# Mamba times mixture of experts: the second expert's rows are weighed and added by one VectorE operation

## The chip, the cores and the metric

The kernel runs on one core of a Trainium2 chip. The core has five engines with a queue each, which work in order and wait for one another by semaphores: PE (TensorE, matrix products), DVE (VectorE), ACT (ScalarE), POOL (GpSimd) and SP (SyncE, which here only issues DMAs). The metric is the device time in microseconds of one execution; less is better. Before the change it is 1489.96 us, the median of three runs from 1489.83 to 1492.37.

## The reference

For 4096 tokens (2 x 2048) of width 256 the reference computes, with everything in fp32:

```
xn = layernorm(x)
s  = xn + mamba(rmsnorm(xn));  s = s + silu(rmsnorm(s) @ w1.T) @ w2.T   # mamba scan, then an MLP
p  = softmax(xn @ gate_w + gate_b); the two best of 8 experts by token
e  = p[first] * expert_first(xn) + p[second] * expert_second(xn)        # relu MLPs, 256-1024-256
out = x + s * silu(e)
```

The Mamba part holds a recurrence over time, h = h * dA + (dt * u) * B, for 512 channels and 16 states, and sums h * C over the states. What matters here is the line with e: two rows of expert output by token, each times its probability, added, and silu of the sum as a gate.

## The kernel before, in words

The tokens are cut into 8 blocks (c) of 512. The Mamba part runs in 256 steps n: for each block 4 groups of 128 channels (d) and 8 pairs of states (g). A step has two half-steps, one state each. In a step VectorE makes b = du * B for both states (L1498) and runs one scan in each half-step (L1502, h); ScalarE makes da by exp for the step two further on (L1387); GpSimd multiplies h by C (L1430) and for most steps adds the two states (L1432); PE adds the result into y three steps later (L1400). At the start of a group VectorE makes du = dt * xc (L1495), with both inputs in SBUF and the output in PSUM.

Everything else is laid between these half-steps. PE's side work (the experts, then the MLP in pieces of 256 tokens) is drawn by an estimate of its time, a fixed amount for each half-step. The evacuations that follow are put off by a list called `later`: `later.put(work, after=k)` runs the work k half-steps on (one without k), and works of the same half-step run in the order in which they were put. So the order on each engine is settled when the program is written, and an engine that stands at a wait holds back all that is behind it.

The experts' outputs lie in DRAM as ys_d. For each of the 16 pieces of 256 tokens of the MLP, `gather` fetches the two rows of each token: four indirect DMAs on GpSimd's queue (L1185), j for the half of the tokens, k for first or second expert, into yk[0] and yk[1], both in SBUF. Five half-steps later `weigh` multiplies the four parts by their probabilities on ScalarE (L1199) and adds yk[1] to yk[0] on GpSimd (L1203). Seven half-steps after the gather `tanh` puts tanh of the half sum into yk[1] on ScalarE (L1207; `prob` already holds the factor one half). At the end of the piece `finish` adds the MLP's product po, in PSUM, to its input (L1218, L1220) and then, in `end`, forms (tanh + 1) * po * yk[0] + x in three VectorE operations (L1228, L1229, L1230; xom is the output piece), which also frees the PSUM bank "o" for PE's next product (pom of the next MLP piece, or po of the Mamba output, L821).

`act_table` (L183) loads ScalarE's table of functions when another than the present one is asked for. exp and tanh share one here; silu has its own. The MLP's silus are gathered (`silus`, L1144) so as to switch less. In the last block the own copy of `yk`, called ykm in the profile, serves the very last piece.

Of the kernel before, what the change touches and what calls it, by code (L numbers as in the profile page):

```python
# [10 lines left out]
AF = mybir.ActivationFunctionType  # L11
ALU = mybir.AluOpType
# [4 lines left out]
NE, FF, TOPK = 8, 1024, 2  # L17
# [11 lines left out]
JS = TS // P  # L29
# [23 lines left out]
def kernel(  # L53
# [18 lines left out]
    nc = tc.nc  # L72
# [107 lines left out]
    def act_table(name):  # L180

        if table[0] != name:
            nc.scalar.preload_act_table_set(name)  # L183
            table[0] = name
# [25 lines left out]
    prob = keep.tile([P, TOPK, NI], F32, tag="prob", name="prob")  # L210
# [145 lines left out]
    later = Later()  # L356
# [19 lines left out]
    def ring(tag, bufs):  # L376

        n = take(tag)
        later.free(tag, n - bufs)
        return tag, n  # L380
# [700 lines left out]
    class Mlp(Ffn):  # L1081
# [82 lines left out]
        def gather(self):  # L1164

            c, hf = self.c, self.hf
            i0 = c * J + hf * JS
            if self.own:
                yk_own = [
                    rows.tile([P, JS, DM], F32, tag="yk", name=f"yk{self.name}_{k}")  # L1170
                    for k in range(TOPK)
                ]
            else:
                yk_taken.append(self.name)
            if not yk_tiles:
                for k in range(TOPK):
                    yk_tiles.append(
                        wpool.tile([P, JS, DM], F32, tag=f"w{k + 1}", name=f"yk{k}", bufs=5)
                    )
            yk = self.yk = yk_own if self.own else yk_tiles  # L1180
            for no in expert_rows:
                later.free(*no)
            for j in range(JS):
                for k in range(TOPK):
                    nc.gpsimd.indirect_dma_start(  # L1185
                        out=yk[k][:, j, :], out_offset=None, in_=ys_d,
                        in_offset=bass.IndirectOffsetOnAxis(
                            ap=row_y[:, k, i0 + j : i0 + j + 1], axis=0
                        ),
                    )  # L1190
            self.nxo = ring("ys", 2)
            self.xo = rows.tile([P, JS, DM], F32, tag="ys", name=f"xo{self.name}")
            self.tok = slice(c * T + hf * TS, c * T + (hf + 1) * TS)
            nc.sync.dma_start(self.xo, x[self.tok, :].rearrange("(j p) d -> p j d", p=P))

            def weigh():
                for j in range(JS):
                    for k in range(TOPK):
                        nc.scalar.activation(  # L1199
                            yk[k][:, j, :], yk[k][:, j, :], AF.Copy,  # L1200
                            scale=prob[:, k, i0 + j : i0 + j + 1],
                        )
                nc.gpsimd.tensor_tensor(yk[0], yk[0], yk[1], ALU.add)  # L1203

            def tanh():
                act_table(WITH_TANH)
                nc.scalar.activation(yk[1], yk[0], AF.Tanh)  # L1207
                self.gated = True

            later.put(weigh, after=5)  # L1210
            later.put(tanh, after=7)

        def finish(self, po, n):
            x1, yk, xo = self.x1, self.yk, self.xo
# [371 lines left out]
```

## Time and profile before

| what | value |
|---|---|
| median of 3 runs | 1489.96 us |
| profiled execution | 1505.4 us, span of its instructions 1503.7 us |
| granted TensorE clock, mean | 0.944 |
| PE, DVE, ACT, POOL busy over the span | 90%, 81%, 65%, 79% |
| first gather of expert rows, last one | 1065.1 us, 1438.6 us |
| ACT table loads | 121 of 1.283 us |
| weighing on ACT (L1199) | 64 operations, 0.50 us each |
| adding on POOL (L1203) | 16 operations, 1.27 us each |
| tanh of the sum on ACT (L1207) | 16 operations, 0.63 us each |

An entry such as "POOL TENSOR_TENSOR h<-h,C 128x1024" names the engine, the operation, the tile written and the tiles read, and the shape as partitions by elements. In rows of groups the number after the bar is busy time in us, then the mean of one in ns, then the idle time of the engine before them and who ended it. In rows of waits the three numbers are us in total, times, and the longest. In rows of the timeline come start, duration, and in brackets the idle time before.

### The profile page before, as it was taken

To read this page: it belongs to the slowest core of one execution; us is meant where nothing else is said; L and a number is where in the kernel's file an instruction comes from. 1 tells how busy PE (TensorE), PEld (TensorE's weight loads), DVE (VectorE), ACT (ScalarE), POOL (GpSimd) and SP (SyncE) were. 2 spreads that over 40 slices of the span, in tenths; PEclk is the share of its full clock that TensorE was granted. 3 is DMA by queue.
4 is the path that set the end of the run, shared out by engine and by line. 5 is a ranking of instruction groups with operands and counts; after the bars stand their busy time and mean duration, and the time that the engine had idled before them with its cause. 6 is when DMAs were issued, how large, how long until landed. Compare 5 with 4: busy or idle time off the path is not lost.

```text
span 1503.7 us, 18025 instructions
## 1 busy us (share of the span) xinstructions
PE 1347.4 (90%) x5122; PEld 944.1 (63%) x5122; DVE 1217.2 (81%) x1351; ACT 978.5 (65%) x1765; POOL 1188.3 (79%) x964
## 2 busy tenths in 40 slices
PE   5744799999999999999999999979878998999958
PEld 4531467765776677766776677546655666667726
DVE  7448888889798998799888988999767967888853
ACT  4742777458655776568656865677648988778932
POOL 2665779987898799968997899889975888777860
PEclk9556899999999999999999999999999999999989
DMA  5568134962477345924492449445830116412110
GB/s 187 198 234 304 46 99 145 306 220 76 125 230 280 92 131 180 335 95 121 158 363 74 129 140 331 167 139 175 268 114 8 55 53 211 139 53 60 57 57 14
DMA packets 169317, 231.85 MB, mean 154 GB/s; under 512 B 19825, under 2 KB 139761, under 8 KB 169217
## 3 DMA queue, kind: packets, MB, share of 16 engines
q1 hardware_dynamic: 163072, 213.91, 42.9%
q0 software_dynamic: 6144, 16.79, 3.4%
q8 instruction: 41, 0.67, 0.2%
q14 instruction: 60, 0.48, 0.1%
HBM read 195.12 MB, written 35.52 MB: 153 GB/s over the span
## 4 chain that ended last, share of the span: by engine, by line
PE 44%; POOL 25%; DVE 10%; ACT 10%; issue 6%; DMA 4%; another core or an unknown queue 1%; POOLq 0%; DVEq 0%; SPq 0%; ACTq 0%
POOL h L1430 13%; PE phe L946 9%; PE y L1400 8%; PE poe L958 8%; POOL h L1432 6%; PE pom L958 4%; PE phm L946 4%; PE po L821 3%; ACT L183 2%; PE px L621 2%; DVE h L1502 2%; DMA B<-bcd 2%; ACT da L1387 2%; PE pz L772 2%; DMA C<-bcd 1%
## 5 line engine op out<-in xcount | busy, mean ns | idle before, releaser
L1430 POOL TENSOR_TENSOR h<-h,C 128x1024 f32<-128x1024 f32 x255 | 604.1, 2371 | 36.7 <-issue 11.5
L1502 DVE TENSOR_TENSOR_SCAN h<-da,hs,b 128x512 f32<-128x512 f32 x384 | 477.6, 1270 | 41.4 <-PE y L1400 10.8
L1387 ACT ACTIVATE da<-dt,a_neg 128x512 f32<-128x512 f32 x512 | 352.8, 717 | 93.3 <-DVE h L1502 87.2
L1400 PE MATMUL y<-h,ident 128*128 128x512 f32 x596 | 307.3, 617 | 34.6 <-POOL h L1432 17.5
L1498 DVE TENSOR_TENSOR b<-du,B 128x1024 f32<-128x1024 f32 x256 | 315.0, 1231 | 18.4 <-DMA B<-bcd 9.1
L1432 POOL TENSOR_TENSOR h<-h 128x512 f32<-128x512 f32 x214 | 275.4, 1287 | 16.8
L946 PE MATMUL phe<-xsTe,w_e 128*128 128x256 f32 (+1 forms) x1248 | 268.1, 366 | 9.4 <-ACT xsTe L937 7.6
L946 PEld LDWEIGHTS phe<-xsTe,w_e 128*128 128x128 f32 x1248 | 225.4, 194 | 72.7 <-issue 27.6
L958 PE MATMUL poe<-w_e,hide 128*128 128x256 f32 x1136 | 265.2, 380 | 2.5 <-ACT hide L1053 2.5
L958 PEld LDWEIGHTS poe<-w_e,hide 128*128 128x128 f32 x1136 | 213.8, 190 | 65.1 <-issue 33.5
L1053 ACT ACTIVATE hide<-phe,b 128x256 f32<-128x256 f32 (+1 forms) x312 | 123.6, 450 | 140.8 <-PE phe L946 140.4
L1400 PEld LDWEIGHTS y<-h,ident 128*128 128x128 f32 x596 | 112.2, 197 | 124.0 <-issue 60.5
L1502 DVE TENSOR_TENSOR_SCAN h<-da,b 128x512 f32<-128x512 f32 x128 | 151.3, 1210 | 12.7 <-PE y L1400 4.8
L183 ACT ACT_TABLE_LOAD x121 | 155.2, 1283 | 2.9 <-PEq L1573 0.8
L946 PE MATMUL phm<-xsTm,w_m 128*128 128x256 f32 x512 | 121.0, 387 | 2.7 <-ACT hidm L1144 2.0
L1424 POOL COPY hs<-h 128x2 f32<-128x2 f32 x192 | 42.0, 219 | 100.9 <-DVE h L1502 89.4
L958 PE MATMUL pom<-w_m,hidm 128*128 128x256 f32 x512 | 121.0, 386 | 0.0
L946 PEld LDWEIGHTS phm<-xsTm,w_m 128*128 128x128 f32 x512 | 99.1, 194 | 29.6 <-issue 10.8
L958 PEld LDWEIGHTS pom<-w_m,hidm 128*128 128x128 f32 x512 | 98.5, 194 | 25.2 <-issue 12.5
L462 POOL DMA_INDIRECT xs_d<-xt,slot x64 | 64.0, 1000 | 49.1 <-issue 21.4
L646 DVE SCALAR_TENSOR_TENSOR xc<-px,par_sb,xc 128x512 f32<-128x512 f32 x96 | 71.6, 748 | 30.4 <-ACT xc L638 25.6
L1185 POOL DMA_INDIRECT yk<-ys_d,row_y x60 | 58.3, 972 | 22.6 <-issue 14.2
(221 smaller groups left out, 1366.7 us busy)
## 6 DMA issues: line engine op xcount, KB each, us to landing
w_e<-in_w SPq DMA_DIRECT2D x312, 256.0 KB
B<-bcd SPq DMA_DIRECT2D x64, 512.0 KB
C<-bcd SPq DMA_DIRECT2D x64, 512.0 KB
xs<-xs_d SPq DMA_DIRECT2D x32, 256.0 KB
ys_d<-ys SPq DMA_DIRECT2D x32, 256.0 KB
b<-in_b SPq DMA_DIRECT2D x39, 128.0 KB
xnr<-xnd SPq DMA_DIRECT2D x16, 256.0 KB
xom<-in_x SPq DMA_DIRECT2D x16, 256.0 KB
```

Source lines behind the costliest of these rows:

```text
L183: nc.scalar.preload_act_table_set(name)
L462: r = nc.gpsimd.indirect_dma_start(out=xs_d, out_offset=bass.IndirectOffsetOnAxis(ap=slot[:, k, i : i + 1], axis=0), in_=x_of(i // J, i % ...
L646: nc.vector.scalar_tensor_tensor(v[:, s : s + T], px, conv_w[:, d, KC - 1 - s : KC - s], v[:, s : s + T], ALU.mult, ALU.add,)
L946: nc.tensor.matmul(ph[:, q, :], self.w1[c0 // 2][:, k, ts(q, P)], self.xT[:, k, :], start=(k == 0), stop=(k == KM - 1),)
L958: nc.tensor.matmul(po[:, j, :], self.hid[c // 2][:, c % 2, ts(j, P)], self.w2[c // 2][:, c % 2, :], start=(c == 0 and j == 0), stop=(c == ...
L1053: nc.scalar.activation(hc[:, q, :], ph[:, q, :], AF.Relu, bias=self.b1[:, c0 + q : c0 + q + 1])
L1387: nc.scalar.activation(das[n][:, q, :], dts[c, d], AF.Exp, scale=a_neg[:, d, 2 * g + q : 2 * g + q + 1])
L1400: nc.tensor.matmul(ys[c, d], ident, hts[n][:, q, :], start=False, stop=(g == DS // 2 - 1 and q == nq - 1),)
L1430: engine.tensor_tensor(hts[n], hts[n], bct[c, "C", g], ALU.mult)
L1432: nc.gpsimd.tensor_tensor(hts[n][:, 0, :], hts[n][:, 0, :], hts[n][:, 1, :], ALU.add)
L1498: nc.vector.tensor_tensor(inp, dus[c, d].unsqueeze(1).to_broadcast([P, 2, T]), bct[c, "B", g], ALU.mult,)
L1502: nc.vector.tensor_tensor_scan(hts[n][:, q, :], das[n][:, q, :], inp[:, q, :], 0.0 if c % CPB == 0 else hs[c - 1][:, d, 2 * g + q : 2 * g ...
```

## The change

`weigh` now multiplies only the first expert's rows on ScalarE. Half a step later a new work `join` multiplies the second expert's rows by their probability and adds them to the first's, in one VectorE operation for each half of the tokens; GpSimd's add is gone. `join` then puts `tanh`, which so runs in the half-step after it. By count that is the same half-step as before, but since it is put later it comes behind other works of that half-step.

```diff
             def weigh():
                 for j in range(JS):
-                    for k in range(TOPK):
-                        nc.scalar.activation(
-                            yk[k][:, j, :], yk[k][:, j, :], AF.Copy,
-                            scale=prob[:, k, i0 + j : i0 + j + 1],
-                        )
-                nc.gpsimd.tensor_tensor(yk[0], yk[0], yk[1], ALU.add)
+                    nc.scalar.activation(
+                        yk[0][:, j, :], yk[0][:, j, :], AF.Copy,
+                        scale=prob[:, 0, i0 + j : i0 + j + 1],
+                    )
+                later.put(join)
+
+            def join():
+                for j in range(JS):
+                    nc.vector.scalar_tensor_tensor(
+                        yk[0][:, j, :], yk[1][:, j, :], prob[:, 1, i0 + j : i0 + j + 1],
+                        yk[0][:, j, :], ALU.mult, ALU.add,
+                    )
+                later.put(tanh)
 
             def tanh():
                 act_table(WITH_TANH)
@@
             later.put(weigh, after=5)
-            later.put(tanh, after=7)
```

The sixteen gathers then carry 32 weighings on ScalarE, 32 operations on VectorE and none on GpSimd. In the built program the order on PE and on SP is unchanged; ScalarE's order differs, beside the 32 missing weighings, at two gathers (the 10th and the 15th), and has two table loads more.

## The prediction

> **What bounds the kernel now.** I read the engine shares and the chain that ended last first, then busy time by stretch, since shares over the whole span mix stages. Only the last third counts: the sixteen gathers of expert rows start at 1065 us.
>
> ```profile
> PE 1347.4 (90%) x5122; PEld 944.1 (63%) x5122; DVE 1217.2 (81%) x1351; ACT 978.5 (65%) x1765; POOL 1188.3 (79%) x964
> 1065.00:1440.00 375.00, 342.93 (x1278) 240.43 (x1276) 297.16 (x282) 295.63 (x454) 297.91 (x235) 0.97 0.30 98
> 1460.00:1503.70 43.70, 33.13 (x145) 27.69 (x144) 14.70 (x29) 11.45 (x27) 0.00 (x0) 0.95 0.04 12
> ```
>
> The numbers behind each stretch are PE, PE weight loads, DVE, ACT, POOL. From 1065 to 1440 PE is busy 91%, the other three 79% each: no engine rules the stretch, the chain changes hands. Only PE's 32 us of idle time, and the tail in which PE waits for POOL, can give anything back. The waits of that stretch say who holds whom:
>
> ```profile
> DVE pom L1218 <- PE pom L958: 24.6, 11, 6.4
> ACT yk L1207 <- POOL yk L1203: 21.7, 10, 6.2
> POOL yk L1203 <- ACT yk L1199: 13.1, 7, 5.9
> PE po L821 <- DVE xom L1230: 10.6, 3, 6.1
> ```
>
> One ring: ScalarE weighs (L1199), GpSimd adds (L1203), ScalarE takes tanh (L1207), VectorE multiplies (L1228), and PE's next product waits for the bank. VectorE itself waits 24.6 us for PE: this is its slack.
>
> **The change part by part.** The working groups of the rows, from the lists by tile and by line:
>
> ```profile
> L1199 ACT ACTIVATE yk<-yk,prob x60: 491/496/510, 1069.8 to 1442.6; 128x256 f32<-128x256 f32 x60
> L1203 POOL TENSOR_TENSOR yk<-yk,yk x15: 1262/1275/1282, 1077.8 to 1451.4; 128x512 f32<-128x512 f32 x15
> L1495 DVE TENSOR_TENSOR du<-dt,xc x32: 673/982/2885, 93.0 to 1407.4; 128x512 f32<-128x512 f32 x32
> L1066 DVE TENSOR_TENSOR ys<-poe,b 128x256 f32<-128x256 f32 x7 | 2.9, 411 | 0.6 <-PE poe L958 0.6
> L567 DVE SCALAR_TENSOR_TENSOR scratch<-scratch,ends x1: 2272/2272/2272, 136.9 to 136.9; 128x8 f32<-128x8 f32 x1
> ```
>
> Removed: 16 GpSimd adds of 1.275 us, 20.4 us of POOL; 32 of 64 ScalarE weighings, and since four overlap to 1.70 us and two to 0.90, 0.80 us a gather, 12.8 us of ACT. Added: 32 VectorE operations on 128x256. The built order of PE and of SP is the same line for line; the gathers keep their places on POOL's queue. So no transfer and no matmul moves by order.
>
> *Price of the VectorE operation.* By L1066 it is 0.41 us. But L1066 reads one operand from PSUM, and the new operation reads both from SBUF. The kernel's recurring VectorE work otherwise avoids that (b, the scan and pom have a PSUM operand); the exception is du, L1495, and its row spreads from 673 to 2885 ns. The longest one beside GpSimd:
>
> ```profile
> 413.85 2.88 DVE L1495 TENSOR_TENSOR du<-dt,xc 128x512 f32<-128x512 f32 x1
> ...
> 413.81 2.37 POOL L1430 TENSOR_TENSOR h<-h,C 128x1024 f32<-128x1024 f32 x1
> 416.26 1.60 POOL L1432 TENSOR_TENSOR h<-h 128x512 f32<-128x512 f32 x1
> ```
>
> du ends 0.55 us after the GpSimd operation that it met, and the next GpSimd operation takes 1.60 for its usual 1.27. L567, a scalar_tensor_tensor of 8 columns, took 2.27 us for the same reason. The Trainium skill (SBUF — State Buffer, "Who interferes with whom") says that a VectorE instruction with two SBUF inputs contends with a GpSimd instruction that reads SBUF and that one fully blocks. That speaks against this change. By the bare row (0.41) the 32 operations cost 13 us of VectorE; by the rule at its worst, each behind a whole 2.37 us operation, 32 x 2.8 = 90 us. The row decides between: du's mean over 32 is 1129 (36.1/32), 0.46 above its undisturbed 0.67. I take 0.41 + 0.46 = 0.87 each, 1.74 a gather, 28 us of VectorE in all. What no row shows is the second of a pair directly after the first: it may pass at once (0.41) or wait for the GpSimd operation queued meanwhile (up to 2.4 more). Both ends are kept. GpSimd loses about 0.3 for each one that it meets. GpSimd's indirect DMAs do not hold it off (du at 93.0 us ran in 0.69 beside one).
>
> *The new wait.* The join stands on VectorE half a step after the weighing on ScalarE, with the recurrence behind it: a scan or b, then GpSimd's h, then da. VectorE runs ahead, so it will stand for the weighing where ScalarE is late. Setting the end of the VectorE instruction before the join against the end of two weighings: about 7 us at the first gather (rows land at 1071.7, VectorE is there at 1064.4), 3 to 5 us at the 5th, 6th, 8th and 10th, at most 2 elsewhere (the 15th would be 5, but its gathers start 2.3 sooner without the add and wait ahead of them, which leaves 0.9). Four of these are covered: VectorE would have waited for PE's pom or y anyway (6.4, 1.6 and 3.6, 3.1 and 4.2, then 2.6 for da). So nothing, with up to 2 us each if the cover is gone; at the 8th it comes out about 2.5 us late into PE's stretch without pause and I count 0 to 1.
>
> *Along the path.* (a) 1077 to 1106: PE waited 6.15 us for xom, behind tanh at 1102.7, behind GpSimd's add. Tanh can now run at 1098 to 1101, but VectorE, nearly without pause since 1079, comes to L1228 at 1101.0 to 1104.7 instead of 1103.4: -2.4 to +1.3, taken -0.6. (b) 1130 to 1142 ScalarE is the chain with the weighing in it: -0.8. (c) 1166 to 1203: the same 0.8, but PE has no pause: 0. (d) At 1216.6 tanh ends ScalarE's longest such wait in the loop:
>
> ```profile
> 1216.62 0.63 ACT L1207 ACTIVATE yk<-yk 128x512 f32<-128x512 f32 x1 [6.17 <-POOL yk L1203]
> 1338.09 1.28 ACT L183 ACT_TABLE_LOAD   x1
> 1339.38 1.08 ACT L1144 ACTIVATE hidm<-phm 128x512 f32<-128x512 f32 x2
> ```
>
> The 6.17 go, but the hidm that follows needs phm, which PE ends at 1217.0 instead of 1219.7: 2.7 are left. ScalarE then is the chain until PE's 3.3 us pause at 1254.6; with 0.8 from the sixth weighing, -3.5. (e) Near 1338 (10th gather) the tanh, now put later, falls behind a silu in the built order: ScalarE has 123 table loads instead of 121. The rows give 1.28 each, with hidm starting 0.01 after the load: 2.57. The skill (ScalarE: Activation LUTs, "What ACT_TABLE_LOAD costs") adds a drain of 1.38 to each switch, 5.3 in all; the row shows no such gap before hidm, so I take 2.57, less 0.8 of weighing: +1.8, since PE waits here for xrm (1.6 us). (f) 1343 to 1404 PE runs without pause: 0, but VectorE, dense too, loses its 2.9 and 2.0 us of slack to three joins and ends some 4.5 behind PE. (g) The tail:
>
> ```profile
> 1445.42 2.46 DVE L1430 TENSOR_TENSOR h<-h,C 128x1024 f32<-128x1024 f32 x1
> ...
> 1451.38 1.26 POOL L1203 TENSOR_TENSOR yk<-yk,yk 128x512 f32<-128x512 f32 x1
> 1452.60 2.34 POOL L1430 TENSOR_TENSOR h<-h,C 128x1024 f32<-128x1024 f32 x1
> ...
> 1455.00 5.25 PE L1400 MATMUL y<-h,ident 128*128 128x512 f32 x8 [2.40 <-POOL h L1430]
> ```
>
> From 1418 to 1455 GpSimd is the chain: three adds (3.8) and a wait for the weighing (1.05) go, up to 2 come back as holds: 1455 becomes about 1452. VectorE, which had 7 us to spare (1447.9 against 1454.9), now arrives at 1447.9 + 1.4 (its lateness after f, net of the -3.1 from a to e) + 0.9 + 0.9 + 1.8 for the last three joins - 0.3 (no wait for tanh) - 1.3 (the hold inside its last operation) = 1451.3. Both near 1451 to 1452, so the y that ended at 1460.3 ends 3 to 5 earlier; the 43 us after it are untouched. These times include the shifts of (a) to (f): the sum is -4.0.
>
> The profiled execution took 1505.4 us (span 1503.7 and 1.7 around it), 15.4 over the median of the runs, 1489.96. Its clock of 0.944 may be the reason; I carry the difference over unscaled: 1489.96 - 4.0 = **1486.0 us**. 0.2% is 3.0 us, about what a measurement here can tell from no change.
>
> **Rivals.** *Slower: VectorE becomes the bound by the shared port.* If the second operation of each pair stands behind the next GpSimd operation (1.0 remaining for the first, then about 1.9), a join costs 3.6 instead of 1.7. At the seven gathers where VectorE is dense (2nd, 8th, 9th, 11th to 13th, 16th) that is 25 us against some 14 of its pauses: +11, +1.8 for the loads, -5 for what still comes off in the ring and the tail: +8, 1498. It decides from about 2.7 us a join. For: du's 2.9; against: many joins meet gathers or an idle GpSimd. *No change: PE covers it.* At 91% busy, PE's pauses may close elsewhere, and the tail's gain is eaten by VectorE's lateness: 1490, within 2. For: (f); against: PE's 7.0 us wait for POOL in the tail. *Larger gain.* All of tanh's waits turn into time (6.2 for PE at 1105, 6 at 1254, 5 in the tail, less the loads and some holds): 1479. Against: VectorE has no room at 1105. *The change does not do what it says*: tanh moves in ScalarE's order only near 1338 and 1440; elsewhere it stands where it was.
>
> **Numbers.** Forecast (-1 to -8) 0.40, of it 0.06 within 0.2%; slower rival 0.30, of it 0.03 within; no change 0.20, of it 0.15 within, 0.03 faster; larger gain 0.10. So faster 0.47, same 0.24, slower 0.29. The range 1480 to 1497 leaves out most of the larger gain and the worst of the slower rival.
>
> **What would show it.** Right: the new VectorE rows at 0.4 minimum and 0.7 to 1.1 mean, tanh's wait for GpSimd (34 us in all) under 10, PE's wait for xom near 1105 not longer, two loads more near 1340, the last GpSimd h ending near 1452. Wrong: a mean over 1.4, PE waits for h or xom that grow, or VectorE's last operation after 1455.

## The result and the profile after

The changed kernel takes 1496.66 us (median of 19 runs, 1491.05 to 1502.57), the kernel before 1491.70 (19 runs on the same chip, 1489.6 to 1493.59): a ratio of 1.0034 [1.0023, 1.0046], 5.0 us slower. Run again on another chip it is 1.0023 [1.0011, 1.0034]. The forecast was 4 us faster. Its range, 1480 to 1497, just held the time; its sign was wrong.

The profiled execution of the changed kernel took 1493.4 us at a clock of 0.951. The shares of the engines on its page:

```profile
PE 1344.8 (90%) x5122; PEld 943.3 (63%) x5122; DVE 1244.6 (83%) x1383; ACT 968.1 (65%) x1735; POOL 1168.0 (78%) x948
```

Over the span VectorE has 27.4 us more, GpSimd 20.3 and ScalarE 10.4 less.

The new operation (minimum, median, maximum in ns) and the table loads of the changed kernel, from its lists by tile and by line:

```profile
L1206 DVE SCALAR_TENSOR_TENSOR yk<-yk,prob,yk x30: 457/980/2570, 1058.7 to 1438.2; 128x256 f32<-128x256 f32 x30
L183 ACT ACT_TABLE_LOAD x123 | 157.8, 1283 | 2.9 <-PEq L1579 0.8
```

With the two of the last piece, 32 operations take 33.9 us, 1.06 each, 2.12 a join. Undisturbed, one takes 0.46. The waits around it from 1052 to 1460 us, which takes in all sixteen gathers:

```profile
ACT yk L1214 <- DVE yk L1206: 24.0, 9, 7.9
DVE yk L1206 <- ACT yk L1198: 22.8, 5, 6.7
PE po L821 <- DVE xom L1236: 9.6, 2, 4.9
```

Over all the gathers tanh waited 34.5 us for GpSimd's add (the 21.7 in the prediction are those up to 1440 us). Now it waits 26.0 us for VectorE's join, the 24.0 here and 2.0 at the last piece: the wait has changed its owner, and three quarters of it are left. VectorE stands 22.8 us for the weighing besides.

**Where the time went.** The two profiled executions cannot be set side by side by the clock on the wall: the one of before came 12.5 us later to the first gathers. So I cut both at the recurrence's own steps (L1508, L1502 before; two scans a step, 256 steps, counted from 0), each time at the end of the step's first scan: A from step 188 to 224 (1st to 7th join), B to step 248 (8th to 13th), C to the end. The numbers behind each stretch are PE, weight loads, VectorE, ScalarE, GpSimd, then clock, DMA share and GB/s. A and B before:

```profile
1056.64:1279.70 223.06, 198.28 (x704) 134.62 (x704) 168.47 (x161) 172.15 (x268) 179.04 (x154) 0.95 0.36 118
1279.70:1410.81 131.11, 125.55 (x495) 91.64 (x494) 109.61 (x104) 107.78 (x163) 102.17 (x70) 1.00 0.24 77
```

After:

```profile
1044.16:1260.36 216.20, 195.74 (x704) 133.59 (x704) 178.87 (x176) 166.60 (x254) 172.23 (x147) 0.96 0.38 121
1260.36:1404.54 144.18, 134.60 (x517) 98.07 (x515) 122.60 (x115) 109.98 (x158) 97.26 (x65) 0.98 0.22 70
```

A is 6.9 us shorter, B 13.1 longer, C 5.8 shorter. The stretch to read is B. It is 13.07 us longer, and VectorE is 12.99 us busier in it. This suggests that VectorE sets the pace there, but it does not show it: the near-equality hangs on the cut (with B ended one step earlier the two are 9.5 and 7.4 us), and PE has 517 matmul records in B for 495, since the cuts follow VectorE and PE's work has moved against them. What VectorE's time is worth in B is shown by the run without the port, below; where PE stands still for it, in the part on why the prediction was wrong.

VectorE's own waits in B, before:

```profile
DVE pom L1218 <- PE pom L958: 10.8, 5, 4.3
```

and after:

```profile
DVE yk L1206 <- ACT yk L1198: 7.2, 2, 4.5
DVE pom L1224 <- PE pom L958: 5.3, 2, 2.9
```

The wait for PE halves, but a wait for the weighing stands beside it: little of VectorE's idle time in B was there to be filled.

The sum A + B + C is 447.06 us before and 447.44 in this profiled execution. The profiled execution of the repeat has 222.1, 144.1 and 87.0, which makes 453.1: B and C are the same to 0.1 us, A is 5.9 longer. So the two profiled executions of the changed kernel take two courses, 0.4 and 6.0 us above that of before; the medians of the runs, 5.0 and 2.7 us above, lie between. What parts them is told at the repeat.

### The profile page after: what moved, and what is told of

It reads as the page before. It is cut to its first block, busy times and chain, and to the rows that moved or that the text cites. A ratio compares the mean times of both kernels' runs of the same rounds, so it can differ in the third digit from the quotient of the medians.

```text
span 1491.6 us, 18074 instructions
## 1 busy us (share of the span) xinstructions
PE 1344.8 (90%) x5122; PEld 943.3 (63%) x5122; DVE 1244.6 (83%) x1383; ACT 968.1 (65%) x1735; POOL 1168.0 (78%) x948
## 5 line engine op out<-in xcount | busy, mean ns | idle before, releaser
L1436 POOL TENSOR_TENSOR h<-h,C 128x1024 f32<-128x1024 f32 x255 | 603.6, 2368 | 46.2 <-DVE h L1508 17.1
L1508 DVE TENSOR_TENSOR_SCAN h<-da,hs,b 128x512 f32<-128x512 f32 x384 | 478.0, 1270 | 32.7 <-PE y L1406 3.7
L1406 PE MATMUL y<-h,ident 128*128 128x512 f32 x596 | 305.0, 612 | 31.8 <-POOL h L1436 18.1
L1438 POOL TENSOR_TENSOR h<-h 128x512 f32<-128x512 f32 x214 | 275.5, 1287 | 16.8
L1053 ACT ACTIVATE hide<-phe,b 128x256 f32<-128x256 f32 (+1 forms) x312 | 123.4, 450 | 140.7 <-PE phe L946 140.5
L1508 DVE TENSOR_TENSOR_SCAN h<-da,b 128x512 f32<-128x512 f32 x128 | 151.3, 1210 | 12.7 <-PE y L1406 4.8
L1430 POOL COPY hs<-h 128x2 f32<-128x2 f32 x192 | 42.5, 221 | 99.6 <-DVE h L1508 96.8
L958 PEld LDWEIGHTS pom<-w_m,hidm 128*128 128x128 f32 x512 | 99.1, 195 | 28.2 <-issue 11.8
```

The lines of the kernel that those rows point to most:

```text
L958: nc.tensor.matmul(po[:, j, :], self.hid[c // 2][:, c % 2, ts(j, P)], self.w2[c // 2][:, c % 2, :], start=(c == 0 and j == 0), stop=(c == ...
L1053: nc.scalar.activation(hc[:, q, :], ph[:, q, :], AF.Relu, bias=self.b1[:, c0 + q : c0 + q + 1])
L1406: nc.tensor.matmul(ys[c, d], ident, hts[n][:, q, :], start=False, stop=(g == DS // 2 - 1 and q == nq - 1),)
L1436: engine.tensor_tensor(hts[n], hts[n], bct[c, "C", g], ALU.mult)
L1438: nc.gpsimd.tensor_tensor(hts[n][:, 0, :], hts[n][:, 0, :], hts[n][:, 1, :], ALU.add)
L1508: nc.vector.tensor_tensor_scan(hts[n][:, q, :], das[n][:, q, :], inp[:, q, :], 0.0 if c % CPB == 0 else hs[c - 1][:, d, 2 * g + q : 2 * g ...
```

## The experiments

All times are medians; each ratio is to the kernel before on the same chip. The first four ran on a chip on which the kernel before takes 1505.99 us, the others where it takes 1490.8 to 1492.7. Forecasts in us that stand ahead of the first four were made for a chip on which it takes 1491.7. A, B, C and VectorE's busy time in B are from each kernel's one profiled execution, cut as above; so a difference of some 6 us in A can be one of course (see the repeat).

| kernel | ratio, 95% interval | A | B | C | VectorE in B | B less VectorE |
|---|---|---|---|---|---|---|
| before | 1 | 223.1 | 131.1 | 92.9 | 109.6 | 21.5 |
| the change | 1.0034 [1.0023, 1.0046] | 216.2 | 144.2 | 87.1 | 122.6 | 21.6 |
| again | 1.0023 [1.0011, 1.0034] | 222.1 | 144.1 | 87.0 | 122.6 | 21.5 |
| tanh in its old order | 0.9983 [0.9974, 0.9992] | 216.2 | 140.5 | 87.2 | 123.4 | 17.2 |
| no port | 0.9926 [0.9913, 0.9940] | 215.9 | 135.2 | 84.6 | 113.1 | 22.1 |
| both | 0.9899 [0.9884, 0.9914] | 216.1 | 132.7 | 84.5 | 113.3 | 19.4 |
| ends alone | 0.9915 [0.9902, 0.9929] | 221.9 | 131.1 | 86.9 | 109.6 | 21.5 |
| middle alone | 1.0078 [1.0064, 1.0092] | 222.6 | 144.3 | 90.4 | 122.6 | 21.6 |
| middle, old order | 1.0040 [1.0026, 1.0054] | 221.0 | 141.5 | 91.6 | 123.4 | 18.1 |
| middle, no port | 1.0020 [1.0012, 1.0028] | 221.7 | 135.4 | 92.2 | 114.4 | 21.0 |
| join half a step later | 1.0005 [0.9993, 1.0017] | 216.8 | 143.5 | 86.0 | 124.7 | 18.8 |
| pair split | 1.0047 [1.0032, 1.0062] | 223.2 | 146.8 | 86.6 | 120.0 | 26.8 |
| one addition | 0.9979 [0.9971, 0.9988] | 221.0 | 137.9 | 87.5 | 113.7 | 24.1 |
| one addition, old order | 0.9960 [0.9946, 0.9973] | 221.8 | 133.0 | 84.9 | 115.3 | 17.7 |
| all but four | 0.9946 [0.9929, 0.9963] | 214.7 | 132.4 | 87.0 | 112.7 | 19.7 |
| all but four, half a step later | 0.9962 [0.9947, 0.9976] | 217.5 | 136.7 | 85.7 | 116.0 | 20.7 |
| all but four, pair split | 0.9994 [0.9984, 1.0003] | 224.1 | 135.9 | 86.5 | 114.1 | 21.8 |
| all but four, one addition | 0.9936 [0.9923, 0.9950] | 222.6 | 130.3 | 86.7 | 110.6 | 19.7 |
| all but four, one addition, old order | 0.9958 [0.9944, 0.9972] | 222.1 | 130.4 | 87.2 | 110.7 | 19.7 |
| before, tanh later | 1.0104 [1.0087, 1.0121] | 228.7 | 137.2 | 96.8 | 108.7 | 28.5 |

**Tanh in its old order.** The join stays on VectorE; tanh is put where it was put before, and runs the join first if it has not run.

```diff
                         yk[0][:, j, :], ALU.mult, ALU.add,
                     )
-                later.put(tanh)
+                self.joined = True
 
             def tanh():
+                while not self.joined:
+                    later.next()
                 act_table(WITH_TANH)
...
+            self.joined = False
             later.put(weigh, after=5)
+            later.put(tanh, after=7)
```

> The change, with tanh put in its old place in the order (121 table loads again instead of 123). Theory A, VectorE's time is the loss (it stands for the weighing and for the GpSimd port in the dense steps after 1215 us): the loads lie beside VectorE's lateness there, so at most 1 us comes off the +5.0: 1495 to 1497. Theory B, the two loads near the tenth gather are on the path: 2 x 1.28 come off, 1493.5 to 1494.5.

1503.36 against 1505.99 us, ratio 0.9983; 121 table loads. A and C are those of the change to 0.1 us; only B is 3.6 shorter, and that with VectorE 0.8 busier. So the new place of tanh has a price of its own, it is paid in B, and the ratio fell by more than either theory gave. ScalarE at the 10th gather in the changed kernel:

```profile
1321.03 1.28 ACT L183 ACT_TABLE_LOAD   x1
1322.33 1.08 ACT L1144 ACTIVATE hidm<-phm 128x512 f32<-128x512 f32 x2
1323.43 1.28 ACT L183 ACT_TABLE_LOAD   x1
1324.72 0.63 ACT L1214 ACTIVATE yk<-yk 128x512 f32<-128x512 f32 x1
1325.37 1.28 ACT L183 ACT_TABLE_LOAD   x1
```

Tanh stands between two silus (L1144, and sz from 1326.67), and both loads around it are extra. From the start of the weighing to xrm, which PE waits for, it is 9.83 us; with tanh in its old order it is 6.96. The difference of 2.87 is the two loads of 1.28 and little else: hidm starts 0.02 after its load has ended. The Trainium skill (ScalarE: Activation LUTs, "What ACT_TABLE_LOAD costs") adds a drain of 1.38 to each, which would have made it 5.3; the measurement decides against it here. What the 2.87 us bring with them lies on PE: it waits 3.61 us for xrm, against 0.75 with the old order, and the 16 products of pom behind that wait take 5.30 us in place of 3.62, at a granted clock of 0.73 from 1328.7 to 1335.0.

**No port.** The VectorE operation takes its third input from PSUM (the recurrence's newest du) in place of SBUF; the first expert's rows are so left out of the sum. It still waits for the weighing.

```diff
                     nc.vector.scalar_tensor_tensor(
                         yk[0][:, j, :], yk[1][:, j, :], prob[:, 1, i0 + j : i0 + j + 1],
-                        yk[0][:, j, :], ALU.mult, ALU.add,
+                        dus[list(dus)[-1]][:, ts(j, DM)], ALU.mult, ALU.add,
                     )
```

> The change, with the VectorE operation reading the current du from PSUM in the place of yk[0] from SBUF, so that only one input lies in SBUF; the first expert's rows are left out of the sum. The order, the wait for the weighing and the table loads stay. Theory A1, the port is the cost: the operation takes 0.41 to 0.47 us each time (mean now 1.06, so 19 us of VectorE less in all), and the time falls below the kernel before: 1482 to 1488. Theory A2, standing for the weighing (22.8 us in five gathers) is the cost: the operation shortens but the time stays within 2 us of the change, 1494 to 1498.

1493.91 against 1505.99 us, ratio 0.9926: theory A1, and a little more than it gave. Its group on the page (busy us, mean ns, idle before it), and its stretch B:

```profile
L1206 DVE SCALAR_TENSOR_TENSOR yk<-yk,prob,du 128x256 f32<-128x256 f32 x30 | 13.0, 473 | 22.6 <-ACT yk L1198 15.7 <-issue 6.1 <-ACT xsTm L937 0.8
1270.98:1406.17 135.19, 127.83 (x498) 93.38 (x497) 113.10 (x115) 105.70 (x153) 95.92 (x65) 0.99 0.24 74
```

The operation falls from 1.06 to 0.47 us, none of the 32 is over 0.48, and B falls by 9.0 us for 9.5 of VectorE: in B the holds come out nearly one to one. This is the shared port, shown by taking one SBUF input away with the order unchanged. The idle time before the operation is still 22.6 us, 15.7 of them put down to the weighing, in a kernel that is faster than the one before: VectorE standing for the weighing is not the main loss.

**At the ends alone, and in the middle alone.** VectorE joins at gathers 1 to 5 and 14 to 16, or at 6 to 13; the others keep ScalarE and GpSimd as before.

```diff
+            n_gathers.append(self.name)
+            by_vector = len(n_gathers) <= 5 or len(n_gathers) >= 14    # middle: 6 <= len(n_gathers) <= 13
...
-                    nc.scalar.activation(
+                    for k in range(1 if by_vector else TOPK):
...
-                later.put(join)
+                if by_vector:
+                    later.put(join)
+                else:
+                    nc.gpsimd.tensor_tensor(yk[0], yk[0], yk[1], ALU.add)
...
             later.put(weigh, after=5)
+            if not by_vector:
+                later.put(tanh, after=7)
```

> The VectorE join only at gathers 1 to 5 and 14 to 16; gathers 6 to 13 weigh and add as before. Theory A: the gain that the traces show up to the scan step 216 (7 us) and in the tail (7 us) stays, and the loss between (15 us) goes: 1478 to 1483. Rival, PE covers: a lead won before 1215 us is lost again where PE runs without pause, and only the tail's part stays: 1484 to 1488.

> The complement: the VectorE join only at gathers 6 to 13. Theory A: no gain ahead and none in the tail, the loss between stays: 1498 to 1506. Rival, PE covers there and the loss comes from the sum of all joins: 1492 to 1495.

1493.34 (0.9915) at the ends, 1517.66 (1.0078) in the middle. The middle alone has the B of the whole change (144.3), the ends alone the B of the kernel before. Both forecasts of theory A hold as ratios: the loss sits in the middle's gathers, and the same edit gains at both ends. In the sum of ratios the change would be at 0.9993; it is measured at 1.0023 to 1.0034, so the two halves are not quite independent.

**The change again.**

> The change itself, beside the same runs of the kernel before as the next three. The first measurement gave a ratio of 1.0034, and the change with tanh in its old place gave 0.9983 on another chip: a distance of 7.6 us for two table loads of 1.28. Theory L, the loads cost what they last on the path: the change lies here 2 to 4 us above what the old tanh place gives, a ratio of 0.999 to 1.001. Rival, the two loads upset the later order and cost three times their time: 1.002 to 1.005.

1495.06 against 1492.41 us, in the rival's range: beside tanh in its old order (0.9983, on another chip) the two loads cost more than twice their time. The two profiled courses part at du (L1501), the VectorE operation with two SBUF inputs that was there before, behind the 1st join. In the course of the first result:

```profile
1069.37 0.72 DVE L1501 TENSOR_TENSOR du<-dt,xc 128x512 f32<-128x512 f32 x1
1070.21 2.36 POOL L1436 TENSOR_TENSOR h<-h,C 128x1024 f32<-128x1024 f32 x1
```

and in the repeat:

```profile
1068.32 2.65 DVE L1501 TENSOR_TENSOR du<-dt,xc 128x512 f32<-128x512 f32 x1
1068.06 2.36 POOL L1436 TENSOR_TENSOR h<-h,C 128x1024 f32<-128x1024 f32 x1
```

In the first, du starts 0.84 us before GpSimd's h and passes in 0.72; in the second, h has started 0.26 us before du, which takes 2.65. So VectorE comes 1.7 us later to the 2nd join (counted from step 188) and meets the next h there: the join takes 3.45 us in place of 1.77, and the repeat stays 4 to 6 us behind from step 196 to the end. In the traces of tanh in its old order and of all but four du takes 0.72 to 0.73 and A is 216.2 and 214.7; in that of the ends alone it takes 2.64 and A is 221.9. The changed kernel's runs spread over 11.5 us, those of before over 4.0; that this lottery is the reason is likely, and not shown.

**The join half a step later,** with tanh right behind it, so that ScalarE's order is the change's.

```diff
-                later.put(join)
+                later.put(join, after=2)
...
-                later.put(tanh)
+                tanh()
```

> The change with only VectorE's join moved half a step back, into the half-step of tanh; ScalarE's order is the same line for line, 123 table loads. Theory A1, the port is the main cost: VectorE stands less for the weighing (23 us in five gathers now, 8 to 16 then), the mean of the operation stays at 1.0 to 1.1, and the time is within 2 us of the change. Theory A2, standing for the weighing is the cost: 4 to 8 us faster than the change.

1492.48 against 1492.41 us, ratio 1.0005. VectorE's standing for the weighing falls from 22.8 to 11.8 us, the holds stay (36.8 us for the 32 operations), and the time falls by 2.6 us against the repeat on the same chip, between the two theories and with intervals that overlap. So 11 us of standing were worth about 3, if anything.

**The kernel before with tanh later by itself.**

```diff
-            later.put(tanh, after=7)
+            later.put(tanh, after=9)
```

> The kernel before, with tanh put 9 half-steps after the gather instead of 7; 119 table loads. No VectorE join. It asks whether the lead of 7 us that the change has at scan step 216 comes from ScalarE no longer standing for GpSimd's add at tanh (34 us before). If so, it comes here too: 3 to 8 us faster than before. Rival, the lead comes from GpSimd's 20 us of adds being gone: within 2 us of before.

1507.24 us, ratio 1.0104 [1.0087, 1.0121], with 119 table loads. Neither theory had that: two loads fewer, and 15 us slower, spread over A, B and C, with VectorE 0.9 us less busy in B. Tanh's place costs more by what waits for it than by its loads. The trace names the wait: PE's waits for xom, which VectorE makes behind tanh, grow from 10.6 to 20.4 us.

**All but four.** VectorE joins except at four gathers of the middle, the 6th, 8th, 10th and 13th, where in the trace of the change it is 9.4, 6.5, 5.4 and 3.8 us from the end of VectorE's operation before the join to the join's end (at eight of the sixteen it is at most 2.0).

```diff
-            by_vector = len(n_gathers) <= 5 or len(n_gathers) >= 14
+            by_vector = len(n_gathers) not in (6, 8, 10, 13)
```

> The VectorE join at all gathers but the 6th, 8th, 10th and 13th, which weigh and add as before: the four at which the join holds VectorE longest in the dense steps (9.4, 6.5, 5.4, 3.8 us from the end of the operation before it to its own end). Theory A with the loss in these four: as fast as with joins at the ends only, a ratio of 0.990 to 0.993. Rival, every join in the dense steps costs its share: 0.994 to 0.998.

1483.37 against 1492.41 us, ratio 0.9946, with 121 loads. Four gathers taken back turn 2.7 us of loss into 9 of gain. This is the rival's range: not all of the loss sat in these four. The 10th is among them, so the two loads and tanh's place there go with the joins.

**The pair split.** Is it the second operation of a pair that pays? Here the recurrence's next instruction stands between the two.

```diff
-            def join():
-                for j in range(JS):
-                    nc.vector.scalar_tensor_tensor(...)
-                later.put(tanh)
+            def join(j):
+                nc.vector.scalar_tensor_tensor(...)
+                if j + 1 < JS:
+                    later.put(lambda: join(j + 1))
+                else:
+                    tanh()
```

> The change with the two VectorE operations of a join put half a step apart: the recurrence's next instruction stands between them, tanh follows the second, ScalarE's order and its 123 table loads are the change's. Theory (the second of a back-to-back pair pays a whole GpSimd operation, because one was queued while the first ran): separated, the mean of the 32 falls from 1.06 us to 0.75 to 0.9, VectorE gets 5 to 10 us back and the time is 3 to 7 us below the change's, ratio to before 0.998 to 1.001. Rival (each operation pays what GpSimd happens to be doing, wherever it stands): the mean stays at 1.0 to 1.1, and the ratio is that of the join put half a step later, 1.0005.

1500.04 against 1491.51 us, ratio 1.0047: no faster than the change, and slower than both theories. The 32 operations take 31.4 us, 0.98 each, near the rival's 1.0. In the change the first of a pair is over 1.2 us 8 times in 16 and the second 6 times; split, 4 and 5 times. No place in the pair is special; each operation pays what GpSimd is doing. And tanh, half a step later again, waits 50.4 us for the join in place of 24.0.

**One addition.** ScalarE weighs both experts' rows as before, VectorE adds them in one operation.

```diff
                 for j in range(JS):
-                    nc.scalar.activation(
-                        yk[0][:, j, :], yk[0][:, j, :], AF.Copy,
-                        scale=prob[:, 0, i0 + j : i0 + j + 1],
-                    )
+                    for k in range(TOPK):
+                        nc.scalar.activation(
+                            yk[k][:, j, :], yk[k][:, j, :], AF.Copy,
+                            scale=prob[:, k, i0 + j : i0 + j + 1],
+                        )
...
-                for j in range(JS):
-                    nc.vector.scalar_tensor_tensor(...)
+                nc.vector.tensor_tensor(yk[0], yk[0], yk[1], ALU.add)
```

> ScalarE weighs both experts' rows as before; VectorE only adds them, in one operation of 128x512 with both inputs in SBUF in place of two of 128x256; the rest as in the change. One meeting with GpSimd in place of two. Theory (price is per meeting, not per element): 0.67 us alone + 0.5 to 0.8 for one meeting, 1.2 to 1.5 a join against the change's 2.1, 16 x 0.7 = 11 us less VectorE time; against it ScalarE has its 12.8 us of weighing back, and VectorE stands for it 0.8 longer a gather. Ratio 1.000 to 1.004. Rival (price goes with the elements moved): a join costs 2.0 to 2.2, the time is above the change's by the weighing, ratio 1.005 to 1.010.

1487.56 against 1491.51 us, ratio 0.9979. The group of the addition:

```profile
L1206 DVE TENSOR_TENSOR yk<-yk,yk 128x512 f32<-128x512 f32 x15 | 18.3, 1218 | 32.0 <-ACT yk L1199 32.0
```

One operation of 512 columns takes 1.22 us, two of 256 took 2.12: the price is paid by the meeting, not by the element. As a ratio it beats the change, though ScalarE has its whole weighing back and VectorE stands 32.0 us for it. The gain was more than either theory gave it.

**Combinations of all but four.** First with the join half a step later and tanh behind it, then with the pair split (the edits are those above).

> VectorE joins except at the 6th, 8th, 10th and 13th gather, which keep ScalarE and GpSimd (121 table loads), and each VectorE join stands half a step later, tanh right behind it. Theory (the join costs where VectorE stands for the weighing or waits for the port): the stands left in this version at the 1st and 5th gather fall by 2 to 3 us, the ratio goes from 0.9946 to 0.992 to 0.995. Rival (a later join makes tanh and the end later by as much): 0.995 to 0.998.

> The same twelve VectorE joins, with the two operations of each half a step apart. Theory (second of a pair pays most): mean of the 24 operations 0.75 to 0.9, ratio 0.991 to 0.994. Rival (place makes no difference to the price): mean 0.95 to 1.1, ratio 0.994 to 0.997.

1485.73 (0.9962 [0.9947, 0.9976]) and 1490.72 us (0.9994 [0.9984, 1.0003]). The later join comes out at its rival's number, but its interval overlaps that of all but four by itself. The split loses again, by more than its rival had; its 24 operations take 1.08 us each.

**What of the middle is port, what is order.** Each taken away in the middle alone, then both everywhere; the edits are those of the first two experiments.

> VectorE joins at the 6th to 13th gather alone (1.0078), now with tanh in the place that ScalarE's order had before the change (121 table loads in place of 123). Theory (the loss in the middle is the port: VectorE's longer joins in a dense stretch): most of it stays, 1.004 to 1.008. Rival (tanh's place near the 10th gather and its two loads are the loss): 0.999 to 1.003.

> VectorE joins at the 6th to 13th gather alone (1.0078), each VectorE operation with its third input in PSUM (a bank of the recurrence) in place of SBUF; the first expert's rows are left out of the sum in these eight gathers. The 123 table loads stay. Theory (port): 8 joins of 0.95 in place of some 2.4 us, 12 us of VectorE less, 0.997 to 1.001. Rival (tanh's place and its loads): the loss stays, 1.004 to 1.008.

> The change with the VectorE operations' third input in PSUM at every gather (the first expert's rows are left out of the sum; 0.9926 so far) and tanh in the place that ScalarE's order had before (121 table loads). If tanh's place has a price of its own, beside the port's: 0.986 to 0.990. If tanh's place only cost what the port's delay made of it, or the old order makes ScalarE stand for the join instead: 0.991 to 0.995.

The middle's 1.0078 falls to 1.0040 with the old order, the edge of what the port alone would leave, and to 1.0020 without the port, between the two theories: both count. With both gone everywhere the ratio is 0.9899, within what a price of its own for tanh's place was given (medians: 1498.98, 1495.93 and 1477.86 against 1492.72 us).

Of the 13.1 us in B, the port's holds are 9.0 (144.2 to 135.2), tanh's place 3.6 (144.2 to 140.5), both together 11.5; 1.6 are left for the operations' bare time of some 5.6 us (12 of 0.47). Of the bare time most was hidden, as forecast; the holds were not.

**Towards a better kernel.** One addition at all but four gathers; one addition everywhere with tanh in its old order; and both.

> VectorE joins except at the 6th, 8th, 10th and 13th gather (121 table loads); ScalarE weighs both experts' rows everywhere, and VectorE's join is one addition of 128x512, one meeting with GpSimd in place of two. Theory (each meeting is paid on the way to the end): from 0.9946 to 0.990 to 0.994. Rival (at these twelve gathers VectorE's time is beside other work, and ScalarE's longer weighing costs): 0.995 to 0.998.

> ScalarE weighs both experts' rows, VectorE adds them in one operation of 128x512 at every gather (0.9979 so far), and tanh has its old place in ScalarE's order (121 table loads). If the price of tanh's place adds to that of the port, as in the last batch (0.3 to 0.5%): 0.992 to 0.996. Rival (ScalarE, which has all its weighing back, now stands for the join in tanh's old place): 0.997 to 1.001.

> The same at twelve gathers, the 6th, 8th, 10th and 13th as before the change (0.9936 with tanh half a step later). The four gathers kept already have the 121 table loads, so theory: tanh's place is worth little more, 0.991 to 0.994. Rival: half a step of tanh costs everywhere, 0.987 to 0.991.

1483.06 (0.9936 [0.9923, 0.9950]), 1484.35 (0.9960 [0.9946, 0.9973]) and 1484.27 us (0.9958 [0.9944, 0.9972]). The first two each met their theory's number; the third missed both, being no better than the second. The best of them is 9.7 us faster than the kernel before (1492.72 on that chip) and beats both kernels, though its interval overlaps that of all but four by itself. One addition with tanh in its old order needs no list of gathers and gives 6.5 (against 1490.83).

## Why the prediction was wrong

*What bounds it.* The prediction found that no engine rules the stretch and took VectorE's 24.6 us of waiting for PE as its slack. An average over 375 us could not show where that slack lies. In B, a third of it, the holds cost 9.0 us for 9.5 of VectorE: there was no slack for them. VectorE's busy time alone does not give B, though. B less that time is 21 to 22 us in eight rows of the table, but 17 to 21 in nine others, 24.1 with one addition, 26.8 with the pair split and 28.5 in the kernel before with tanh later.

*The price of one operation: nearly right.* Forecast 0.41 alone and 0.46 for the port, 0.87 each and 28 us in all; measured 0.46 to 0.47 alone, 0.59 for the port, 1.06 each and 33.9 in all. The Trainium skill's rule (SBUF — State Buffer, "Who interferes with whom") was weighed and the port was counted. The rule also says that an operation with at most one SBUF input does not contend, outside the two-port modes; the run without the port agrees, with 473 ns. How a hold looks, at the 8th gather in the changed kernel:

```profile
1264.00 1.27 POOL L1438 TENSOR_TENSOR h<-h 128x512 f32<-128x512 f32 x1
1264.22 3.84 DVE L1206 SCALAR_TENSOR_TENSOR yk<-yk,prob,yk 128x256 f32<-128x256 f32 x2 [2.69 <-ACT yk L1198]
1265.23 2.54 POOL L1436 TENSOR_TENSOR h<-h,C 128x1024 f32<-128x1024 f32 x1
```

The first operation ends after L1438 (1265.27), the second, 2.57 long, after L1436 (1267.77). This is the open end that the prediction kept ("or wait for the GpSimd operation queued meanwhile"); it came six times in sixteen.

*The step that failed: what the holds cost the path.* The 28 us were priced on VectorE and then put at next to nothing on the way to the end: "0 to 1" at the 8th gather, where VectorE was seen 2.5 us late, and in (f) "0", with VectorE "some 4.5 behind PE" carried to the tail only. PE's order is the same in both kernels, so each of its instructions can be timed in both traces. Its lateness against the kernel before, in us, both counted from step 188:

| PE up to (clock of before) | forecast | the change | again | no port | tanh in its old order | both |
|---|---|---|---|---|---|---|
| 1255, behind (a) to (d) | -4.9 | -7.2 | -1.1 | -6.1 | -7.2 | -5.9 |
| 1340, behind the 8th and 9th join | -4.9 to -3.9 | -3.3 | +2.5 | -5.8 | -3.2 | -5.6 |
| 1347, behind (e) | -3.1 | +0.5 | +6.2 | -3.8 | -4.0 | -6.4 |
| 1415, behind (f) | -3.1 | +0.5 | +6.2 | -3.8 | -4.0 | -6.4 |
| 1434 | | +5.9 | +11.6 | -3.5 | +2.4 | -6.0 |
| the end | -4.0 | +0.4 | +6.1 | -11.4 | -3.2 | -13.9 |

The pauses behind two of these rows, in the changed kernel:

```profile
1292.32 5.36 PE L821 MATMUL po<-ow_sb,sz 128*128 128x256 f32 x16 [4.85 <-DVE xom L1236]
1406.64 1.99 PE L958 MATMUL pom<-w_m,hidm 128*128 128x256 f32 x8 [2.36 <-DVE xom L1236]
1418.80 2.07 PE L1402 MATMUL y<-xc,ddiag 128*128 128x512 f32 x2 [2.41 <-DVE sz L1414]
```

and the same three before:

```profile
1309.54 3.69 PE L821 MATMUL po<-ow_sb,sz 128*128 128x256 f32 x16 [3.21 <-DVE xom L1230]
1416.11 1.89 PE L958 MATMUL pom<-w_m,hidm 128*128 128x256 f32 x8
1425.60 1.02 PE L1396 MATMUL y<-xc,ddiag 128*128 128x512 f32 x2
```

Around the 8th and 9th join PE loses 4.0 and 3.5 us in the two traces; without the port it is 0.3. In (f) itself PE loses nothing, as forecast, but VectorE's lateness comes out right behind it, in two waits for VectorE where there were none: PE loses 5.4 us there in both traces, 0.3 without the port. A part of both is PE's clock. Behind the wait of 4.85 the 16 products take 5.36 us for 3.69, at a granted clock of 0.68 from 1292.3 to 1297.7 (1.00 for them before), and it is 0.69 from 1418.8 to 1424.0. Why the clock falls behind one wait and not another is open: without the port these 16 take 5.38 behind a wait of 3.15.

*(e), mis-sized.* +1.8 for two loads net of 0.8 of weighing; on PE it is 3.7 in both traces. With tanh in its old order it is -0.8: that is 4.5 for tanh's place, 2.86 of waiting for xrm and 1.68 of lower clock behind it. Without the port the clock stays at 1.00 there and it is 2.1.

*(a) to (d), unsteady.* -4.9 was forecast; -7.2 and -1.1 came, on either side. (b) is -0.8 in the first, as forecast. What parts the two is du and the 2nd join (see the repeat), which the prediction did not price by itself.

*(g), near by luck.* From 1404 us to the end -0.9 was forecast, and -0.1 came, out of two larger parts that cancel: +5.4 behind (f) and -5.5 in the tail. The chain of the tail in the changed kernel:

```profile
1443.44 1.22 DVE L1436 TENSOR_TENSOR h<-h,C 128x1024 f32<-128x1024 f32 x1
...
1441.95 1.98 PE L1406 MATMUL y<-h,ident 128*128 128x512 f32 x4 [1.37 <-POOL h L1436]
1444.72 1.98 PE L1406 MATMUL y<-h,ident 128*128 128x512 f32 x4 [0.80 <-DVE h L1436]
```

GpSimd's last h (ends at 1441.89) comes 397.7 us after the cut at step 188, 398.3 before: 0.6 earlier, not 3. VectorE's last one ends at 1444.66, which is 1457.1 on the clock of before (12.48 later), where the prediction had 1451.3. PE's last wait for an h is for VectorE's. GpSimd's adds were gone from the tail as forecast, and PE's longest wait for h fell from 7.0 to 2.5 us; VectorE's lateness took that back.

*The standing for the weighing: right.* Some 7 us at the 1st gather and 3 to 5 at four others were forecast; 6.7, 2.9, 6.0, 2.7 and 4.5 came, and they cost little by themselves: the kernel without the port keeps 15.7 us of them and is 0.9926, and 11 us less were worth about 3.

*The rivals.* "VectorE becomes the bound by the shared port" is nearest to what happened, 1498 against 1496.7. But its price was 3.6 us a join and its point of decision 2.7, and 2.1 was enough (2.4 in B): the point was set as if VectorE's pauses at seven gathers could be used up first.

*The signs.* The new rows are as listed, the two loads too; tanh's 34 us for GpSimd are gone, as listed, and are 26 for VectorE. Two signs of being right failed: GpSimd's last h ends at 1454.4 on the clock of before, not near 1452, and PE's wait for xom near 1105, 6.15 us before, is 4.78 in one course but 7.91 in the other. Of the signs of being wrong, VectorE's last operation after 1455 showed, at 1457.1, and PE's waits for xom grew, from 10.6 to 12.0 us, while those for h fell from 14.4 to 8.8 between the first gather and the tail. The mean of 1.06 did not reach 1.4. A sign that looks at one operation missed where the time went; the lateness of the engine whose order is unchanged shows it.

## What to carry to other kernels

Before work is moved to an engine, cut the trace at the loop's own steps and look where that engine is densest: in B its idle time was no reserve for the holds, though most of the bare time was hidden. Where an engine's order stays the same, subtract the times of its instructions in the two traces, one by one: each jump names a wait, or a fall of the clock behind a wait. An operation with both inputs in SBUF beside a busy GpSimd is priced by how often it meets a GpSimd instruction: here one wide operation was cheaper than two narrow ones, 1.22 us against 2.12, and narrow ones with an input in PSUM cheaper still, 0.47 each. Moving a step by half a turn also moves it among the table loads; count them, and what waits for it, apart from the work that was moved.

## What was not expected

- Tanh later by itself, with nothing else changed and two table loads fewer, made the kernel before 15 us slower.
- The same program took two courses 6 us apart, which part at one VectorE operation that comes 0.84 us ahead of a GpSimd instruction or 0.26 us behind it.
- The profiled execution of before was 15.4 us over the median that the prediction had. The prediction supposed the clock; the traces show that it came to step 188 12.5 us later than that of the changed kernel, 11.7 of them in the first 100 us, which the change does not touch.
